# Where the bias products, the weights and the first strips stand in a four-layer network of involutions and convolutions

## The chip, the cores and the metric

The kernel runs on one core of one Trainium2 chip. The metric is the device time of one execution of the whole program, in microseconds (us), as the median of several runs. A core has TensorE (PE in the profile), VectorE (DVE), ScalarE (ACT), GpSimd (POOL) and SyncE (SP). Each takes its instructions in order from a queue of its own; ScalarE, GpSimd and SyncE also issue the DMA transfers here. PSUM holds what TensorE computes until another engine has read it ("evicted" it).

## The reference, cut to what matters

Four layers work on `x`, (4, 256, 56, 56) in fp32. Each normalizes its input and adds its result to it.

```python
x = x + L0(_gn(x))   # involution, 7x7, 16 groups
x = x + L1(_gn(x))   # two 3x3 convolutions
x = x + L2(_gn(x))   # involution, 7x7, 16 groups
x = x + L3(_gn(x))   # gate from Fourier transforms

def _gn(v, G=32, eps=1e-5):            # 32 groups of 8 channels
    g = v.reshape(B_, G, C_ // G, H_, W_)
    return ((g - mean(g)) / jnp.sqrt(var(g) + eps)).reshape(v.shape)

def L0(x):                             # one 7x7 filter for every pixel
    h = einsum('bchw,oc->bohw', x, reduce_w) + reduce_b        # 256 -> 64
    kern = einsum('bchw,oc->bohw', h, span_w) + span_b         # 64 -> 16 * 49
    return (kern * patches(x, 7, 7)).sum(over the 49 taps)

def L1(x):
    h = relu(bn(conv3x3(x, w1), ...))
    return relu(x + bn(conv3x3(h, w2), ...))

def L2(x):                             # as L0, with batch norms and ReLU
    t = relu(bn1(einsum('bchw,oc->bohw', x, w1)))
    wgt = einsum('bchw,oc->bohw', t, w2) + b2
    return relu(bn2((wgt * patches(x, 7, 7)).sum(over the 49 taps)))
```

## The kernel before

**Tiles.** A unit is one image and one half of the channels: 128 channels on the partitions, 56 x 56 pixels. There are eight units, taken in order. All four layers are one program. Layers 0 and 2 come from `involution_layer`, layer 1 from `conv_layer`; layer 3 is folded into layer 2's pass. The tile scheduler is bound to the order of the program text on each engine by `in_order`, so instructions of one engine run as the text issues them.

**An involution's unit.** `bottleneck` (for the first image of layer 0: `begin`) computes the 64 values `h` for each pixel: products of the image with `redn`, the reduction weights times the norm's scale (L459, in layer 0 L529), evicted by ScalarE into `hp` with the bias `hb` (L478, L566). The bias comes from a small product of `red_sb`, the unscaled weights, with the norm's shift (L437). Then `tap_matrices` makes a banded matrix for each group: 32 groups of 36 products (L580). Every third group is evicted by ScalarE (L591, with bias tables `zb_sb`), the others by VectorE (L598). The loop has *hooks*: after group n, the listed steps of other work are issued. Last, `apply` multiplies, for each of 7 columns of pixels, the matrices with the windows of the image (L622).

The windows come from `next_strip` and `next_windows`. `next_strip` normalizes a column's strip of the image into the only `strip_sb`: GpSimd in layer 0 (L381), ScalarE in layer 2 (L379). `next_windows` transposes it on TensorE (seven products, L396), ScalarE copies the result (L408), and SyncE and GpSimd issue copying DMAs (L414, L416). At the first unit of a layer three columns are made ahead of `apply`. Before, the first strip is issued after `bottleneck`, and the pairs of window and next strip at hooks 2, 7 and 12 of the matrices.

**The start of layer 0 (`begin`).** The images' first two halves are loaded by SyncE. The biases `sb` of the filters, the span weights and `red_sb` are loaded by GpSimd's queue. `window_biases` turns the biases into the table `zb_sb`: 24 products of 16 columns each (L255) and a copy by ScalarE (L262). Then come the first half's statistics (VectorE) and norm, `norm_steps`: aggregate the statistics (L204), average over 8 channels by a product with `gavg` (L207, twice), scale and shift. `warm` issues products whose results nobody reads. Products of the first half (L529, 0) go ahead of the second half's norm, those of the second half follow. The 20 evictions by L566 come next, then the matrices.

**The start of layer 1.** The convolutions are computed in a transformed domain: along x, six positions k for four outputs. `row_weights` makes the six weight sets from the three columns of the filter, in two halves of the input channels; per half there are three operations on VectorE for the sums and differences (u2, u1, u2) and three for the positions 3 and 4 (u4, u3, u4). It is a generator: each `next` issues one part. `weights1` is the first convolution's, `weights2` the second's. `phases` (L1290, ScalarE) normalizes a chunk of rows, `transform` (L1293 to L1317, VectorE) makes the six inputs, and `load_rows` loads the next chunk's rows. At the start of the layer the order on each engine is:

- VectorE: the six operations of sums and differences, four steps of the transform, the six other weight operations, the eight remaining steps;
- TensorE: 24 products of `window_biases` for layer 2 (L255), then the convolution (L1411);
- ScalarE: eight phases, then the copy of the bias table.

**The pass of layer 1.** Twelve chunks of rows (three of each image) go through the first convolution (`conv1`: L1411, or L1382 for positions 1 to 3 of all chunks but the first) and the second (`conv2`: L1493) in the order (1,0), (1,1), (2,0), (1,2), (2,1) and so on. Each chunk has a list `after` of what VectorE and ScalarE are to do behind which position: the transform of the next chunk's input (`input2` ends at L1318), outputs and sums. The five parts of `weights2` are placed in the first two chunks; `(2, 0)` is the chunk that first reads them. The last chunk's list calls `begin_last`, which loads the first image of layer 2.

**The start of layer 2.** `red_sb` is a tile of each involution layer's own pool, and in layer 2 it is loaded by ScalarE's queue (L317) when that pool opens, which is after the convolutions. `bottleneck(0)` scales it into `redn`, makes `hb` and the products, and the matrices follow.

Of the kernel before, what the change touches and what calls it, by code (L numbers as in the profile page):

```python
# [10 lines left out]
F32 = mybir.dt.float32  # L11
# [5 lines left out]
P = 128  # L17
# [54 lines left out]
def net_kernel(  # L72
# [59 lines left out]
    for i in range(2):  # L132
        nc.scalar.dma_start(rp[i * R : (i + 1) * R, :], rpar)
    mhalf = const.tile([P, NB], F32, name="mhalf")
# [89 lines left out]

    def mark():
        return len(nc.cur_bb.bb.instructions)
# [23 lines left out]
    def window_biases(zb_sb, bias, ps):  # L250

        bias_f = bias[:G, KK * KK : KK * KK + ZN]
        for p in range(TP):
            z0 = ZF - p // TX * QX - p % TX
            nc.tensor.matmul(  # L255
                ps[:Q, p * G : (p + 1) * G],
                bias_f[:, z0 : z0 + Q],
                ident_sb[:G, :G],
                start=True,
                stop=True,  # L260
            )
        nc.scalar.copy(  # L262
            zb_sb.rearrange("q g p -> q p g"), ps[:Q, : TP * G].rearrange("q (p g) -> q p g", g=G)
        )
# [15 lines left out]
    def involution_layer(layer, xin, xout, red, span, sb, xs_of, ahead=None, pending=None):  # L280

        with ExitStack() as es:
# [12 lines left out]
            def warm(n, by):  # L295

                ps = one_bank()
                for _ in range(n):
                    nc.tensor.matmul(ps[:, :P], ident_sb, by, start=True, stop=True)
# [11 lines left out]

            red_sb = wpool.tile([P, NB, 2, R], F32, name="red_sb")

            def load_red():
                for i in range(2):
                    eng = nc.gpsimd if layer == 0 else nc.scalar
                    eng.dma_start(red_sb[:, :, i], red.rearrange("(cb p) r -> p cb r", p=P))  # L317

            if layer == 2:
                load_red()  # L320
# [41 lines left out]
            def next_strip():  # L362

                if len(strips) == len(columns):
                    return
                b, cb, tx = columns[len(strips)]
                rstd, shift = (t[:, cb : cb + 1] for t in norms[layer][b])
                st = strip_sb
                strips.append(st)
                lo, hi = max(0, tx * TX - PAD), min(W, tx * TX + TX + PAD)  # L370
                at = lo - (tx * TX - PAD)
                if at > 0:
                    nc.vector.memset(st[:, PAD : PAD + H, 0:at], 0.0)
# [47 lines left out]
            def bottleneck(b):  # L421
# [64 lines left out]
            def begin():  # L486
# [4 lines left out]
                biases = bias_table(scratch[:, n:], sb, nc.gpsimd.dma_start, nc.scalar.copy)  # L491
# [3 lines left out]
                load_red()  # L495
# [9 lines left out]
                redn = work.tile([P, NB, 2, R], F32, name="redn", bufs=1)  # L505
                rstd, shift = norms[0][0]
                steps(sums0, NCHUNK)
                norm = norm_of(0, 0, 0, sums_of[0, 0])
                steps(norm, 2)
                warm(4, ident_sb)  # L510
                steps(norm, 2)
                warm(8, ident_sb)
# [7 lines left out]


                pairs = [two_banks() for _ in range(4)]
                bank = pairs[3][:, 1, :]
# [34 lines left out]
                for j in range(NH):  # L558
                    products(j, 1)
                for j in range(NH):  # L560
# [3 lines left out]
                    for py in range(min(rows, TY)):  # L564
                        dst = hp[:, py, :, a0 : a0 + n, :]
                        nc.scalar.activation(dst, s[:, py, :, :n, :], AF.Identity, bias=hb)  # L566
                return folds
# [587 lines left out]
    def conv_layer(xin, xout, st, ahead):  # L1155
        with ExitStack() as es:
# [44 lines left out]
            def row_weights(u, wc, raw=None):  # L1201
# [520 lines left out]
```

## Time and profile before

| | |
|---|---|
| median of 3 runs | 1817.9 us (1817.29 to 1822.03) |
| the profiled execution | 1812.46 us |
| its span | 1810.7 us |
| mean granted clock of TensorE | 0.979 |
| busy: TensorE, VectorE, ScalarE, GpSimd | 1720.8, 1375.4, 842.2, 430.0 us |
| products of the matrices, L580, and of the windows, L622 | 392.1 and 379.0 us |
| products of the second convolution, L1493 | 385.0 us |
| products of the first convolution, L1411 and L1382 | 212.3 and 98.6 us |
| layer 0 | 0 to 507 us |
| layer 1 | 507 to 1240 us |
| layers 2 and 3 | 1240 to 1811 us |

The span is that of one profiled execution, from its first instruction to its last; the runs are other executions of the same program, without a profile. Busy times of different engines overlap. The clock is what the chip granted TensorE: 1.00 is full speed, 0.50 half of it. The layers' bounds are read from the timeline: the first product of layer 1's biases starts at 507.1 us, the last product of the second convolution ends at 1240.2 us.

### The profile page before, as it was taken

What the parts mean: (1) busy time and instruction counts of PE and PEld (TensorE: products, weight loads), DVE (VectorE), ACT (ScalarE), POOL (GpSimd) and SP (SyncE); (2) the same over time, 40 slices, a digit from 0 to 9 for tenths busy, and PEclk for the clock granted to TensorE, in tenths of its full rate; (3) what the DMA queues carried; (4) which work ended last, traced back from release to release, by engine and by line L of the source; (5) the groups of instructions that cost most, each with busy time, mean ns of one, the idle gap of its engine ahead of it and who ended that gap; (6) DMA issues with size and microseconds to landing.
All of it is one profiled execution on the core that took longest, in us unless ns stands there. A gap on an engine that the chain in (4) does not pass through costs nothing.

```text
span 1810.7 us, 55835 instructions
## 1 busy us (share of the span) xinstructions
PE 1720.8 (95%) x24034; PEld 1514.9 (84%) x24034; DVE 1375.4 (76%) x2729; ACT 842.2 (47%) x1981; POOL 430.0 (24%) x626
## 2 busy tenths in 40 slices
PE   7999999999989999999999999997999999899988
PEld 6998989889878988998899889985988887887876
DVE  3787777776689988898889888875777677677775
ACT  3566556555532322322232222113767567577564
POOL 2333433245210000000000000000000374563572
PEclk9999999999989999999999999998999999999997
DMA  2545534454651201120121111031534566665653
GB/s 85 158 154 165 164 119 143 159 159 116 209 174 49 69 26 63 63 70 30 59 73 59 41 60 34 34 135 49 161 132 149 168 218 188 202 210 168 169 156 127
DMA packets 66004, 215.77 MB, mean 119 GB/s; under 512 B 13237, under 2 KB 20926, under 8 KB 62046
## 3 DMA queue, kind: packets, MB, share of 16 engines
q1 hardware_dynamic: 48718, 145.24, 25.7%
q0 software_dynamic: 14688, 64.78, 11.3%
q8 instruction: 190, 3.11, 0.7%
q10 hardware_dynamic: 2352, 2.18, 0.4%
q14 instruction: 56, 0.46, 0.1%
HBM read 76.30 MB, written 49.15 MB: 69 GB/s over the span
## 4 chain that ended last, share of the span: by engine, by line
PE 76%; DVE 9%; ACT 6%; DMA 4%; issue 2%; POOL 2%; SPq 1%; ACTq 0%; POOLq 0%; DVEq 0%
PE mm L1493 19%; PE ps L580 18%; PE ps L622 14%; PE mm L1411 10%; PE mm L1382 5%; PE ps L396 5%; DMA xw<-xw 4%; ACT kt L591 3%; PE ps L459 2%; DVE un L642 1%; DVE kt L598 1%; ACT xw L408 1%; ACT hp L478 1%; SPq L414 1%; DVE res L1486 1%
## 5 line engine op out<-in xcount | busy, mean ns | idle before, releaser
L580 PE MATMUL ps<-hp,z_sb 64*126 64x133 f32 x6144 | 392.1, 281 | 16.2 <-ACT kt L591 7.0
L622 PE MATMUL ps<-kt,xw 126*32 126x48 f32 (+1 forms) x12544 | 379.0, 236 | 24.1 <-DMA xw<-xw 12.1
L622 PEld LDWEIGHTS ps<-kt,xw 126*32 126x32 f32 (+1 forms) x12544 | 341.9, 122 | 68.2 <-issue 46.3
L580 PEld LDWEIGHTS ps<-hp,z_sb 64*126 64x126 f32 x6144 | 369.1, 187 | 34.6 <-ACT kt L591 12.7
L598 DVE TENSOR_TENSOR kt<-ps,zb_sb 126x798 f32<-126x798 f32 x336 | 319.8, 981 | 90.1 <-PE ps L580 89.5
L1493 PE MATMUL mm<-v,u_sb 128*128 128x280 f32 (+1 forms) x1728 | 385.0, 385 | 3.4 <-DVE v L1318 3.4
L1493 PEld LDWEIGHTS mm<-v,u_sb 128*128 128x128 f32 x1728 | 327.9, 190 | 57.5 <-DVE v L1318 3.8
L591 ACT ACTIVATE kt<-ps,zb_sb 126x133 f32<-126x133 f32 x1056 | 306.9, 442 | 96.2 <-PE ps L580 95.6
L1411 PE MATMUL mm<-v,u_sb 128*128 128x252 f32 (+1 forms) x936 | 212.3, 388 | 3.4 <-DVE v L1302 3.4
L1411 PEld LDWEIGHTS mm<-v,u_sb 128*128 128x128 f32 x936 | 178.3, 192 | 33.8 <-issue 3.5
L1530 POOL DMA_DIRECT2D x<-xs x24 | 13.1, 546 | 683.2 <-DVE xs L1529 427.4
L642 DVE SCALAR_TENSOR_TENSOR un<-ps,s,un 128x240 f32<-128x240 f32 x224 | 102.5, 457 | 85.7 <-ACT un L637 81.5
L642 DVE SCALAR_TENSOR_TENSOR un<-ps,par_sb,un 128x240 f32<-128x240 f32 x224 | 98.3, 457 | 87.1 <-ACT un L635 82.8
L1478 ACT ACTIVATE res<-xs,shift,norm_sb 128x1120 f32<-128x1120 f32 (+1 forms) x24 | 30.2, 1259 | 236.3 <-DVE xs L1529 107.3
L408 ACT COPY xw<-ps 126x896 f32<-126x896 f32 x112 | 101.4, 906 | 47.9 <-PE ps L396 37.7
L647 POOL TENSOR_TENSOR xs<-un,xs 128x240 f32<-128x240 f32 x112 | 72.3, 664 | 192.4 <-DVE un L642 192.3
L396 PE MATMUL ps<-ident_sb,strip_sb 128*126 128x128 f32 x784 | 111.7, 283 | 6.1 <-POOL strip_sb L381 5.8
L635 ACT ACTIVATE un<-ps,par_sb 128x240 f32<-128x240 f32 x112 | 50.1, 448 | 115.7 <-PE ps L622 113.4
L1382 PE MATMUL mm<-xs,u_sb 128*128 128x126 f32 (+1 forms) x792 | 98.6, 277 | 1.3 <-DVE xs L1345 0.9
L396 PEld LDWEIGHTS ps<-ident_sb,strip_sb 128*126 128x126 f32 x784 | 84.9, 142 | 17.0 <-POOL strip_sb L381 6.9
L637 ACT ACTIVATE un<-ps,bn_t,s 128x240 f32<-128x240 f32 x112 | 60.0, 538 | 83.3 <-PE ps L622 72.1
L1382 PEld LDWEIGHTS mm<-xs,u_sb 128*128 128x128 f32 x792 | 94.5, 191 | 2.4 <-issue 1.0
(254 smaller groups left out, 1925.8 us busy)
## 6 DMA issues: line engine op xcount, KB each, us to landing
xw<-xw SPq DMA_DIRECT2D x168, 252.0 KB
xw<-xw SPq DMA_DIRECT2D x224, 126.0 KB
xw<-xw POOLq DMA_DIRECT2D x56, 252.0 KB, 4.7
xs<-x SPq DMA_DIRECT2D x24, 560.0 KB
x<-xs POOLq DMA_DIRECT2D x8, 1568.0 KB, 8.2
xs<-x SPq DMA_DIRECT2D x8, 1568.0 KB
xs<-in_x_dram SPq DMA_DIRECT2D x6, 1568.0 KB
x<-xs SPq DMA_DIRECT2D x6, 1568.0 KB
```

Of the source, the lines that this page charges most:

```text
L396: nc.tensor.transpose(ps[:Q, k * P : (k + 1) * P], flat[:, k * Q : (k + 1) * Q], ident_sb)
L408: nc.scalar.copy(xw[:, :NSB, :], ps[:Q, : NSB * P].rearrange("q (n c) -> q n c", n=NSB))
L580: nc.tensor.matmul(ps[:Q, i, k * NT : (k + 1) * NT], z_sb[i * R : (i + 1) * R, cb * GB // 2 + gp, z0 : z0 + Q], hp[i * R : (i + 1) * R, py ...
L591: nc.scalar.activation(kt[:, g0 + i, pb, :, k], ps[:Q, i, k * NT : (k + 1) * NT], AF.Identity, bias=zb_sb[:, cb * GB + g0 + i, p0 + k : p0 ...
L598: nc.vector.tensor_tensor(kt[:, g0 : g0 + 2, pb], ps[:Q, :, : PB * NT].rearrange("q i (k t) -> q i t k", k=PB), zb_sb[:, cb * GB + g0 : cb ...
L622: nc.tensor.matmul(v[m * j : m * j + m, i, :, k * TP : (k + 1) * TP], xw[:, window(ty), m * j : m * j + m], kt[:, ng * j : ng * j + ng, :, ...
L637: nc.scalar.activation(part, o[0], AF.Identity, bias=bn["t4"][:, cb : cb + 1], scale=bn["s4"][ng][:, 0, cb : cb + 1])
L642: nc.vector.scalar_tensor_tensor(part, o[e], s, part, ALU.mult, ALU.add)
L647: nc.gpsimd.tensor_tensor(dst, u, dst, ALU.add)
L1382: nc.tensor.matmul(ps[:, co * m : (co + 1) * m], u[ci][:, co * P : (co + 1) * P], v2[:, e, : n // 2, ci * WT : (ci + 1) * WT], start=(ci = ...
L1411: nc.tensor.matmul(ps, u1_sb[:, ci, dy, k, co * P : (co + 1) * P], v[:, k, dy * NB + ci : (dy + n - 1) * NB + ci + 1 : NB, :], start=(j == 0),
L1493: nc.tensor.matmul(ps, u2_sb[:, ci, dy, k, co * P : (co + 1) * P], v[:, k, dy * NB + ci : (dy + n - 1) * NB + ci + 1 : NB, :], start=(j == 0),
```

## The change

In layer 0, `window_biases` becomes a generator that yields after each product. 14 of the 24 products stay ahead of the first norm. Ten are issued after the products of the second half (L529), and the copy into `zb_sb` after the evictions into `hp`. The four PSUM pairs are taken earlier, and the bias products use the part of the last pair's second bank behind its first columns. The biases are loaded by ScalarE's DMA queue instead of GpSimd's.

`red_sb` is now a tile of the pool of constants, loaded for layer 2 by SyncE's queue at the start of layer 1 (`begin_conv`). Its scaled copies `redn` are constants too, and those of layer 2's first image are made in `begin_last`.

In layer 2, the first strip is issued ahead of `bottleneck(0)`, and two pairs of window and next strip ahead of the matrices; the third pair is at hook 7. The first two strips are made by GpSimd.

In `row_weights` the first sums of both halves come first, then both subtractions as a part of their own, then the positions 3 and 4. It now has six parts instead of five. For the first convolution, the part with the subtractions is issued after three steps of the transform; the second convolution's parts are called at the same places as before, so that the last of them falls at the end of chunk (1, 1).

After the bias products at the start of layer 1 come three products of 448 columns whose results nobody reads, and `load_rows(1)` follows them; they read the tile that it overwrites.

```diff
+    red_sb = const.tile([P, NB, 2, R], F32, name="red_sb")
+
+    def load_red(red, eng):
+        for i in range(2):
+            eng.dma_start(red_sb[:, :, i], red.rearrange("(cb p) r -> p cb r", p=P))
+
+    def new_redn():
+        return const.tile([P, NB, 2, R], F32, name="redn")
...
+    redn_of = {}
+    def norm_weights(layer, b):
+        redn = redn_of[layer, b] = new_redn()
+        for ci in range(NB):
+            nc.vector.tensor_scalar_mul(redn[:, ci], red_sb[:, ci], norms[layer][b][0][:, ci : ci + 1])
@@ window_biases @@
                 start=True,
                 stop=True,
             )
+            yield
         nc.scalar.copy(
@@ involution_layer @@
-            red_sb = wpool.tile([P, NB, 2, R], F32, name="red_sb")
-
-            def load_red():
-                for i in range(2):
-                    eng = nc.gpsimd if layer == 0 else nc.scalar
-                    eng.dma_start(red_sb[:, :, i], red.rearrange("(cb p) r -> p cb r", p=P))
-
-            if layer == 2:
-                load_red()
@@ next_strip @@
-                if layer == 2:
+                if layer == 2 and len(strips) > 2:
                     nc.scalar.activation(dst, img, AF.Identity, bias=shift, scale=rstd)
                 else:
                     nc.gpsimd.tensor_scalar(dst, img, rstd, shift, ALU.mult, ALU.add)
@@ bottleneck @@
-                rstd, shift = norms[layer][b]
-                redn = work.tile([P, NB, 2, R], F32, name="redn", bufs=1)
-                for ci in range(NB):
-                    nc.vector.tensor_scalar_mul(redn[:, ci], red_sb[:, ci], rstd[:, ci : ci + 1])
+                _, shift = norms[layer][b]
+                if (layer, b) not in redn_of:
+                    norm_weights(layer, b)
+                redn = redn_of[layer, b]
@@ begin @@
-                biases = bias_table(scratch[:, n:], sb, nc.gpsimd.dma_start, nc.scalar.copy)
+                biases = bias_table(scratch[:, n:], sb, nc.scalar.dma_start, nc.scalar.copy)
...
-                window_biases(zb_sb, scratch[:, n:], one_bank())
+                pairs = [two_banks() for _ in range(4)]
+                bank = pairs[3][:, 1, :]
+                biases = window_biases(zb_sb, scratch[:, n:], bank[:, R:])
+                steps(biases, 14)
...
                 for j in range(NH):
                     products(j, 1)
+                steps(biases, TP - 14)
...
                         nc.scalar.activation(dst, s[:, py, :, :n, :], AF.Identity, bias=hb)
+                run(biases)
                 return folds
@@ the hooks of the first unit @@
                 nc.sync.dma_start(zb_sb, zb2_dram)
+                next_strip()
                 run(bottleneck(0))
                 hooks0[3] = list(pending[0])
-            next_strip()
-            for i in range(NXW):
-                hooks0.setdefault(2 + 5 * i, []).extend((next_windows, next_strip))
+                for _ in range(NXW - 1):
+                    next_windows()
+                    next_strip()
+                hooks0[7] = [next_windows, next_strip]
+            if layer == 0:
+                next_strip()
+                for i in range(NXW):
+                    hooks0.setdefault(2 + 5 * i, []).extend((next_windows, next_strip))
@@ begin_conv @@
         raw_weights(1, 0, 1, nc.sync)
+        load_red(red2, nc.sync)
@@ row_weights @@
                 for w0, w1, w2, u1, u2, u3, u4 in ws:
                     tt(u2, w0, w2, ALU.add)
                     tt(u1, u2, w1, ALU.add)
+                    yield
+                for w0, w1, w2, u1, u2, u3, u4 in ws:
                     tt(u2, u2, w1, ALU.subtract)
-                    yield
+                yield
@@ conv_layer @@
-            window_biases(zb2, room["bias"], one_bank())
+            run(window_biases(zb2, room["bias"], one_bank()))
             nc.sync.dma_start(zb2_dram, zb2)
+
+            ps = one_bank()[:, : CR * W]
+            for _ in range(3):
+                nc.tensor.matmul(ps, ident_sb, room["rows"][:, : CR * W], start=True, stop=True)
             load_rows(1, xin)
             g = input1(0)
-            for _ in range(4):
+            for _ in range(3):
                 next(g)
+            next(weights1)
+            next(g)
             run(weights1)
@@ begin_last @@
             load_block(blocks[0, cb], src[2][0][cb])
+        norm_weights(2, 0)
```

More of the change, by code (lines that the diff above doesn't have):

```diff
@@ L293, in one_bank, with warm @@
                 return two_banks()[:, 0, :]
-            def warm(n, by):
-                ps = one_bank()
+            def warm(n, by, ps=None):
+                if ps is None:
+                    ps = one_bank()
                 for _ in range(n):
@@ L494, in begin @@
                 next(tables)
-                load_red()
+                load_red(red, nc.gpsimd)
                 hp = new_h().rearrange("p (y x a t) -> p y x a t", y=TY, x=TX, t=NTX)
@@ L501, in begin @@
                 run(tables)
-                window_biases(zb_sb, scratch[:, n:], one_bank())
+                pairs = [two_banks() for _ in range(4)]
+                bank = pairs[3][:, 1, :]
+                biases = window_biases(zb_sb, scratch[:, n:], bank[:, R:])
+                steps(biases, 14)
                 folds = batch_norms()
                 sums0, sums1 = sums(0, 0), sums(0, 1)
-                redn = work.tile([P, NB, 2, R], F32, name="redn", bufs=1)
+                redn = new_redn()
                 rstd, shift = norms[0][0]
                 steps(sums0, NCHUNK)
-                norm = norm_of(0, 0, 0, sums_of[0, 0])
+                norm = norm_steps(sums_of[0, 0], lambda: bank, 0, 0, 0)
                 steps(norm, 2)
-                warm(4, ident_sb)
+                warm(4, ident_sb, pairs[3][:, 0, :])
                 steps(norm, 2)
-                warm(8, ident_sb)
+                warm(8, ident_sb, pairs[3][:, 0, :])
                 steps(norm, 1)
@@ L519, in begin @@
                 steps(sums1, NCHUNK - 4)
-                pairs = [two_banks() for _ in range(4)]
-                bank = pairs[3][:, 1, :]
                 norm = norm_steps(sums_of[0, 1], lambda: bank, 0, 0, 1)
```

## The prediction

> **What bounds the kernel now.** I read the page first, for the bound, and then the timeline and the windows at the four places that the diff touches.
>
> ```profile
> span 1810.7 us, 55835 instructions
> PE 1720.8 (95%) x24034; PEld 1514.9 (84%) x24034; DVE 1375.4 (76%) x2729; ACT 842.2 (47%) x1981; POOL 430.0 (24%) x626
> PE 76%; DVE 9%; ACT 6%; DMA 4%; issue 2%; POOL 2%; SPq 1%; ACTq 0%; POOLq 0%; DVEq 0%
> L1493 PE MATMUL mm<-v,u_sb 128*128 128x280 f32 (+1 forms) x1728 | 385.0, 385 | 3.4 <-DVE v L1318 3.4
> ```
>
> TensorE is the bound: what is saved where TensorE waits, or runs slowly, shifts all that follows it. The last line has the one wait of the second convolution, 3.4 us for VectorE (L1318).
>
> **A, the first norm.** The timeline of the first 45 us (start, length, engine, line):
>
> ```profile
> 1.50 0.69 POOL L244 DMA_DIRECT2D xs<-in_sb_dram  x1 [0.20 <-issue]
> 6.97 0.23 ACT L247 COPY xs<-xs 16x49 f32<-16x49 f32 x1 [2.58 <-DMA xs<-in_sb_dram]
> 7.26 10.42 PE L255 MATMUL ps<-ident_sb,xs 16*126 16x16 f32 x48 [7.26 <-ACT xs L247]
> 10.39 0.34 DVE L204 BATCH_NORM_AGGREGATE mv<-st 128x2 f32<-128x42 f32 x1
> 17.61 0.59 PE L207 MATMUL ps<-mv,gavg_sb 128*128 128x1 f32 x2
> 32.90 5.75 ACT L566 ACTIVATE hp<-ps,hb 128x168 f32<-128x168 f32 x20 [14.09 <-PE ps L529]
> 38.60 3.75 PE L580 MATMUL ps<-hp,z_sb 64*126 64x133 f32 x36 [2.15 <-ACT hp L566]
> ```
>
> The statistics are ready at 10.73, but their product L207 stands behind 24 bias products until 17.61. A bias product is two records, 10.42/24 = 0.434 us. The change leaves 14 ahead: 10 x 0.434 = 4.34 us less.
>
> It also moves the load of the biases from GpSimd's queue to ScalarE's, where it is issued after the table load and the copy that ends at 4.39, and waits for the first x transfer (its statistics began at 4.58). In that queue the trace's packets go strictly one transfer after the other: the last rp packets run to 8.0 to 8.2, and this load is behind them. Bounds: it lands as before (0) or some 2.2 us later, L247 at 9.2. I take 2.0, because the queue's packets show that order. GpSimd issues the span loads 0.69 us earlier; ScalarE's copies of them (8.84 to 12.1) slip at most 0.5 us, and nobody reads them until 38.6. The second half of x: one of its transfers now waits for cp, the next for rp, so they start some 1 us later; they landed by 14.2 and are first used at 20.44, which becomes 18.1. Hidden.
>
> The 10 others come after the products of L529, which end at 36.46. TensorE waits there until 38.60; at full clock a bias product is 0.22 us (507.1 to 510.3), so 2.2 us fill the 2.15. The copy into zb_sb (1.10 us, L262) now stands on ScalarE between hp and the first eviction, where 1.13 us were idle (39.78). Both covers are just long enough; without them it would be 2.2 and 1.1. **A: 4.34 - 2.0 = -2.3** (-4.3 to -0.7, the last if a window of half clock falls differently, 1.4).
>
> **B, the start of the convolutions.**
>
> ```profile
> 508.11 6.62 ACT L1290 ACTIVATE ph<-xs,norm_sb 128x294 f32<-128x294 f32 x8 [1.68 <-POOL xs L647]
> 515.44 0.80 DVE L1298 SCALAR_TENSOR_TENSOR v<-ph 128x616 f32<-128x616 f32 x1
> 517.93 37.19 PE L1411 MATMUL mm<-v,u_sb 128*128 128x280 f32 x144 [3.37 <-DVE v L1302]
> ...
> 510.33:513.74 3.41, 3.41 (x18) 3.41 (x18) 3.31 (x5) 3.41 (x5) 0.00 (x0) 0.50 1.04 421
> 520.57:523.98 3.41, 3.41 (x9) 2.50 (x8) 3.34 (x4) 0.07 (x1) 0.00 (x0) 0.50 0.36 147
> 523.98:527.40 3.42, 3.42 (x16) 2.71 (x16) 3.39 (x6) 0.32 (x1) 0.00 (x0) 1.00 0.02 5
> ```
>
> In the windows the last three columns are granted clock, DMA share, GB/s. The clock falls to half at 510.33, under the narrow bias products, and returns at 523.98, after one window filled with wide ones. The two subtractions (L1220, 0.985 us each) go behind L1302, but L1298 also needs ScalarE's last phase (514.73): it starts at 514.8, 0.65 us earlier, and everything behind the subtractions is 1.97 - 0.65 = 1.3 us later. The three wide products are 448 columns; L1411 has 280 in 0.934 us a pair at half clock, so 1.49 each, 4.5 us, ending at 518.9: TensorE starts some 1 us later, but with the clock back one window sooner, and is about 1.2 us earlier by 527. That is not kept: VectorE is busy 9.7 of 10 us here, the next conv1 chunk waits for its L1345 at 556.0, and on the way it has 0.41 and 0.96 us of waits for TensorE, which take up its 1.3. The load of the next rows now waits for the wide products, 2.4 us later; its reader waits at 527.97 for VectorE. **B: 0** (-0.3 to +1).
>
> A page speaks of this place otherwise. The Trainium skill (TensorE: Matmul & The Clock Gate, "HAM oscillation") says to allow no idle gaps over some 3.4 us; TensorE is listed as busy under the bias products and still loses the clock, so the measurement goes ahead of the rule. By the rule the wide products would run at full clock, and B would still be 0, VectorE being the bound.
>
> **D, the second convolution's weights.** Before, all twelve weight operations (0.95 to 0.985 us each) stand ahead of L1318, for which TensorE waits 587.2 to 590.87. After, three of them (those of the second half of the channels) are behind it: L1318 ends at 590.8 - 2.95 = 587.9. The product then needs the moved weights for its second half: they start after L1434 (591.86 - 2.95 = 588.9) and the needed one is done 1.94 later, 590.85. Three pairs of 0.377 run 587.95 to 589.1, three from 590.9 to 592.05. ScalarE's copy of that product is at 594.59 before. Of these 2.5 us, 1.4 depend on the window of half clock 592.25 to 595.66: bounds -1.1 to -3.1 with it and without. **D: -1.9**; L1440 and what follows on VectorE keep their times, as the number of operations is the same.
>
> **C, the start of the last involution.**
>
> ```profile
> 1243.13 0.99 ACTq L317 DMA_DIRECT2D red_sb<-in_red_dram  x2
> 1247.04 0.99 PE L437 MATMUL ps<-norm_sb,red_sb 128*128 128x1 f32 x4 [6.81 <-DMA red_sb<-in_red_dram]
> 1247.95 7.42 PE L459 MATMUL ps<-xs,redn 128*64 128x504 f32 x28
> 1251.47 8.34 ACT L478 ACTIVATE hp<-ps,hb,bn_s 64x168 f32<-64x168 f32 x20 [19.30 <-PE ps L459]
> 1259.64 4.36 PE L580 MATMUL ps<-hp,z_sb 64*126 64x133 f32 x36 [4.27 <-ACT hp L478]
> ```
>
> The weights are loaded when the place is free and land 4 us later. After, they and their scaled copy are there since the convolutions: two issues (0.99) on SyncE at 464, where it waits 15 us for its next (cover gone: +1), and two scalings (0.48) on VectorE in a chunk with slack. L437 then waits only for the last PSUM read, L1524, done at 1240.71; products 1240.8 to 1247 run beside VectorE, at full clock, since the 6.8 us gap is gone. What is late next is the bias hb on VectorE: L1529 ends at 1244.40, two norm steps 0.14, memset 0.20, hb 0.22: 1245.1 against ScalarE's 1251.47, so -6.35. GpSimd's first strip (0.89) runs then too; L547 took 0.85 us beside L381 where its equal L516 took 0.28, so up to 0.57 back, I take 0.25: -6.1.
>
> The matrices up to 1289.7 are 30.1 us. TensorE's own work in them is 32 groups of 0.738 (60 records in 3.69) and four sets of transposes of 0.98: 27.5, so 2.6 are lost to half clock and waits. After, two sets stand ahead of it: 25.6. Two strips leave ScalarE (0.93, 1.04), but two window copies and a strip (0.91, 0.91, 1.04) are now queued ahead of its first eviction, which comes 1.3 us later after hp than before. Loss 0 to 3.9; I take 2.6 again, the nearest row: 28.2, -1.9. GpSimd's last output DMA goes 0.9 us later, read 300 us after. **C: -8.0** (-6.4 to -10.8).
>
> Against C stands the skill's same page, "PE-mode transpose": transposes do not count as busy for the clock. No row here shows them alone. By it the 14 transposes would not hold the clock and the loss would be nearer 3.4: C -7.2.
>
> **Sum:** -2.3 + 0 - 1.9 - 8.0 = -12.2. The profiled execution took 1812.46 us (span 1810.7 and 1.76 around it), which gives 1800.3. Its time is 5.4 under the median of 1817.9; I take the sum from the median: **1805.7**.
>
> **Rivals.** R1, the gains are partly given back: A -1.0, B +1.0, D -0.5 (the wait moved to the weights), C -6.4: -6.9, 1811.0. For it: ScalarE is busy 25.0 of 30.1 us in the matrices, VectorE 9.7 of 10 in B. Against it: the cover rows above. R2, slower: in the last involution TensorE starts the matrices at half clock, ScalarE's late evictions keep opening gaps, and no 3.41 us window is full, so that the clock does not return. A group costs 1.43 instead of 0.738; all 32 give +20 on C, 1825.7; it decides from 18 groups on (12.2/0.69). For it: at the end of the kernel the page shows PEclk 7 in the last slice. Against it: 36 records at half clock were enough twice (39.3 to 42.7, 1257.8 to 1264.7) to bring it back, as TensorE at half clock is itself the bound. R3, the change does not do what it says: L437 still waits for something of the convolution until 1247; C is the 0.5 of the scalings: -4.7, 1813.2. The order of the built program speaks against it.
>
> **Chances.** Forecast 0.72, R1 0.14, R3 0.06, R2 0.08. About 0.3% (5.5 us) is what a measurement can tell from no change; the runs before span 0.26%. Faster: 0.72 and 0.08 of R1, 0.80; same: R3 and the rest of R1, 0.12; slower: R2, 0.08. The best bounds give -18, the worst without a rival -6; with R1 and R3 inside and R2 left out: 1800 to 1814.
>
> **What would show it.** A: L207 near 15.3 and L580 near 36.4. B: L1411 at about the same distance from the bias products, clock back a window sooner, L1382 not earlier than A brings it. D: L1493's wait for L1318 under 1 us and a second one for the weights. C: no gap before L437, ScalarE's hp some 6 us earlier. Wrong would be a later L580 in A (the bias load), or half clock for more than two windows after hp in C.

## The result, and the profile after

| | before | changed |
|---|---|---|
| median of 8 runs each | 1818.01 us (1814.48 to 1826.22) | 1812.55 us (1806.19 to 1815.32) |
| profiled execution | 1812.46 us | 1815.32 us |
| ratio of the runs | | 0.9962, 95% interval 0.9942 to 0.9981 |

The change saves 5.5 us by the medians and 6.9 by the ratio (3.5 to 10.5 by its interval); 12.2 were forecast. One execution of both_again (below) took 9300 us, far from the other five, and is left out of the figures. The two profiled executions alone would mislead: that of the kernel before is faster than each of its eight runs, that of the changed kernel is its slowest. So I read the traces stage by stage. Times are from the span's start, in us.

| | before | changed | difference |
|---|---|---|---|
| first matrices of layer 0 start | 38.60 | 44.09 | +5.5 |
| layer 0's last window product ends | 505.90 | 511.10 | +5.2 |
| second convolution starts | 582.64 | 586.87 | +4.2 |
| its second chunk starts | 641.38 | 643.56 | +2.2 |
| convolutions end | 1240.23 | 1242.39 | +2.2 |
| first eviction into `hp`, layer 2 | 1251.47 | 1247.09 | -4.4 |
| first window products, layer 2 | 1289.63 | 1281.52 | -8.1 |
| end of the span | 1810.70 | 1813.55 | +2.9 |

In the changed program the line numbers are 10 to 22 higher: L255 is L273, L207 L217, L299 (the warming products) L319, L529 L540, L566 L578, L580 L593, L1493 L1515, L1318 L1340, L437 L447, L459 L469, L478 L488. In the kernels of the experiments some are a few lines higher still (L1518 and L1511 are L1515 and L1508 here).

**A** went the wrong way. The timeline of the changed kernel (start, length, engine, line; in brackets the idle time before it and what ended it):

```profile
4.82 0.35 ACTq L262 DMA_DIRECT2D xs<-in_sb_dram  x1
10.80 0.23 ACT L265 COPY xs<-xs 16x49 f32<-16x49 f32 x1 [6.41 <-DMA xs<-in_sb_dram]
11.09 6.14 PE L273 MATMUL ps<-ident_sb,xs 16*126 16x16 f32 x28 [11.09 <-ACT xs L265]
17.16 0.59 PE L217 MATMUL ps<-mv,gavg_sb 128*128 128x1 f32 x2
17.61 2.05 PE L319 MATMUL ps<-ident_sb 128*128 128x128 f32 x8
19.70 0.16 DVE L220 COPY gm<-ps 128x1 f32<-128x1 f32 x1 [8.31 <-PE ps L319]
20.94 3.56 PE L319 MATMUL ps<-ident_sb 128*128 128x128 f32 x16
24.54 0.16 DVE L148 TENSOR_SCALAR norm_sb<-ps 128x1 f32<-128x1 f32 x1 [4.09 <-PE ps L319]
...
34.06 7.24 PE L540 MATMUL ps<-xs,redn 128*128 128x504 f32 x14 [0.39 <-DVE hb L568]
41.23 2.37 PE L273 MATMUL ps<-ident_sb,xs 16*126 16x16 f32 x20
43.63 0.51 ACT L578 ACTIVATE hp<-ps,hb 128x56 f32<-128x56 f32 x2 [0.59 <-PE ps L273]
44.09 3.22 PE L593 MATMUL ps<-hp,z_sb 64*126 64x133 f32 x30 [0.49 <-ACT hp L578]
```

The biases' load is issued at 4.82 and its reader starts at 10.80, against 6.97 before. Its 16 packets of 196 bytes ran from 8.55 to 9.64 (before 5.37 to 6.20), behind those of `rp`, which ended at 8.87, much as the prediction had it; but its reader came 1.2 us after the last of them. The fourteen products give back what the load lost (L217 at 17.16, before 17.61). But then VectorE's copy of the average waits, not for the average, done at 17.75, but for L319, the first four warming products (two records each), which nobody reads; the second time it is the eight others, for which L148 waits until 24.54, while before it started at 20.36. The last eviction, too, waits for bias products that it does not read. The warming products, the averages, the bias products and the last rows' products (7th of seven) now all lie in one PSUM tile of two banks.

**D** and **C** went as forecast or better. The waits of TensorE from 586 to 644 us (line, what it waited for, total, times, longest):

```profile
PE mm L1515 <- DVE u_sb L1246: 1.5, 1, 1.5
...
PE mm L1515 <- DVE v L1340: 0.4, 1, 0.4
```

The 3.4 us for the transform have become 0.4, and 1.5 for the weights that were moved behind it. The start of layer 2 in the timeline:

```profile
1243.02 0.58 PE L447 MATMUL ps<-norm_sb,red_sb 128*128 128x1 f32 x4 [0.63 <-DVE xs L1546]
1243.52 5.92 PE L469 MATMUL ps<-xs,redn 128*64 128x504 f32 x28
1246.75 0.20 DVE L383 MEMSET strip_sb<- 128x168 f32 x1
1246.87 0.10 DVE L458 SCALAR_TENSOR_TENSOR hb<-ps,bn_s,bn_t 128x1 f32<-128x1 f32 x1
1247.09 8.33 ACT L488 ACTIVATE hp<-ps,hb,bn_s 64x168 f32<-64x168 f32 x20 [12.76 <-DVE hb L458]
...
1252.30 0.96 PE L406 MATMUL ps<-ident_sb,strip_sb 128*126 128x128 f32 x7 [1.64 <-ACT hp L488]
...
1255.26 7.46 PE L593 MATMUL ps<-hp,z_sb 64*126 64x133 f32 x96 [2.00 <-ACT hp L488]
...
1280.61 0.98 PE L406 MATMUL ps<-ident_sb,strip_sb 128*126 128x128 f32 x7
```

The gap of 6.8 us ahead of L447 is 0.63. ScalarE now waits for the bias `hb`, which stands on VectorE's queue behind the strip's edge (L383). The matrices take 25.4 us up to the last set of transposes (L406 at 1280.61), against 29.1.

### The profile page after: what moved, and what is told of

It reads as the page before. It is cut to its first block, busy times and chain, and to the rows that moved or that the text cites. A ratio compares the mean times of both kernels' runs of the same rounds, so it can differ in the third digit from the quotient of the medians.

```text
span 1813.6 us, 55844 instructions
## 1 busy us (share of the span) xinstructions
PE 1723.7 (95%) x24040; PEld 1514.2 (83%) x24040; DVE 1376.3 (76%) x2729; ACT 840.2 (46%) x1979; POOL 430.8 (24%) x627
## 3 DMA queue, kind: packets, MB, share of 16 engines
q1 hardware_dynamic: 49262, 145.37, 25.6%
## 4 chain that ended last, share of the span: by engine, by line
PE 73%; DVE 12%; ACT 5%; DMA 4%; issue 3%; POOL 2%; SPq 1%; POOLq 0%; ACTq 0%; DVEq 0%
PE mm L1515 18%; PE ps L593 18%; PE ps L635 14%; PE mm L1433 9%; PE mm L1404 5%; PE ps L406 5%; DMA xw<-xw 3%; ACT kt L604 2%; DVE un L655 2%; PE ps L469 1%; DVE kt L611 1%; DVE res L1508 1%; DVE xs L1367 1%; SPq L424 1%; ACT xw L418 1%
## 5 line engine op out<-in xcount | busy, mean ns | idle before, releaser
L635 PE MATMUL ps<-kt,xw 126*32 126x48 f32 (+1 forms) x12544 | 381.1, 236 | 31.9 <-issue 20.2
L635 PEld LDWEIGHTS ps<-kt,xw 126*32 126x32 f32 (+1 forms) x12544 | 342.4, 122 | 77.5 <-issue 54.2
L593 PE MATMUL ps<-hp,z_sb 64*126 64x133 f32 x6144 | 391.3, 281 | 10.1 <-ACT kt L604 6.1
L593 PEld LDWEIGHTS ps<-hp,z_sb 64*126 64x126 f32 x6144 | 369.6, 187 | 27.7 <-ACT kt L604 12.0
L1515 PE MATMUL mm<-v,u_sb 128*128 128x280 f32 (+1 forms) x1728 | 383.5, 383 | 1.9 <-DVE u_sb L1246 1.5
L1515 PEld LDWEIGHTS mm<-v,u_sb 128*128 128x128 f32 x1728 | 326.1, 189 | 56.3 <-DVE u_sb L1246 1.9
L406 PE MATMUL ps<-ident_sb,strip_sb 128*126 128x128 f32 x784 | 113.6, 286 | 8.3 <-POOL strip_sb L391 5.2
L406 PEld LDWEIGHTS ps<-ident_sb,strip_sb 128*126 128x126 f32 x784 | 86.6, 144 | 19.3 <-POOL strip_sb L391 8.3
```

Source lines behind the costliest of these rows:

```text
L406: nc.tensor.transpose(ps[:Q, k * P : (k + 1) * P], flat[:, k * Q : (k + 1) * Q], ident_sb)
L593: nc.tensor.matmul(ps[:Q, i, k * NT : (k + 1) * NT], z_sb[i * R : (i + 1) * R, cb * GB // 2 + gp, z0 : z0 + Q], hp[i * R : (i + 1) * R, py ...
L635: nc.tensor.matmul(v[m * j : m * j + m, i, :, k * TP : (k + 1) * TP], xw[:, window(ty), m * j : m * j + m], kt[:, ng * j : ng * j + ng, :, ...
L1515: nc.tensor.matmul(ps, u2_sb[:, ci, dy, k, co * P : (co + 1) * P], v[:, k, dy * NB + ci : (dy + n - 1) * NB + ci + 1 : NB, :], start=(j == 0),
```

## The experiments

The ratio is to runs of the kernel before on the same chip, with its 95% interval. The stages are compared in the traces, one execution each. In programs that are equal up to there, the first matrices of layer 0 start within 0.5 us of each other (35.99 to 36.49), but layer 0 ends within 1.9 (501.81 to 503.67); the later parts vary more, as the last experiment shows. The runs were taken on several chips, and the intervals of most of these kernels overlap: the parts are told apart by the stages, not by the medians.

| | median | ratio |
|---|---|---|
| a_undone | 1806.21 | 0.9930 (0.9910 to 0.9950) |
| warm_other_pair | 1807.62 | 0.9937 (0.9917 to 0.9957) |
| load_gpsimd | 1809.87 | 0.9948 (0.9927 to 0.9968) |
| both_mended | 1801.39 | 0.9906 (0.9883 to 0.9929) |
| both_again, the same program | 1807.50 | 0.9930 (0.9908 to 0.9953) |
| m_no_idle | 1804.15 | 0.9931 (0.9907 to 0.9954) |
| m_old_strips | 1799.91 | 0.9915 (0.9881 to 0.9948) |
| m_strips_act | 1803.25 | 0.9937 (0.9915 to 0.9960) |
| m_red_late | 1807.27 | 0.9932 (0.9906 to 0.9958) |
| m_old_w2 | 1807.48 | 0.9935 (0.9909 to 0.9961) |
| m_plus | 1800.55 | 0.9926 (0.9900 to 0.9952) |
| m_hb_first | 1795.47 | 0.9869 (0.9841 to 0.9897) |

### The start of layer 0 as before (a_undone)

```diff
-                bias_table(scratch[:, n:], sb, nc.scalar.dma_start, nc.scalar.copy)
+                bias_table(scratch[:, n:], sb, nc.gpsimd.dma_start, nc.scalar.copy)
...
-                steps(biases, 14)
+                run(window_biases(zb_sb, scratch[:, n:], one_bank()))
...
-                warm(8, ident_sb, pairs[3][:, 0, :])
+                warm(8, ident_sb)
```

> The changed kernel with the start of layer 0 as it was before (biases on GpSimd's queue, all 24 products ahead of the first norm); B, C and D stay. Theory W (the start of layer 0 costs 5.5 us, as the stage times of the two traces have it): the first matrices start at 38.6 instead of 44.1 us, and the median is 5.5 us under the changed kernel's, about 1807. Rival P (the forecast's -2.3 holds and the profiled execution of the changed kernel was only an unlucky one): the median is 2.3 us above the changed kernel's, about 1815.

The matrices start at 39.70 us, 4.4 earlier than in the changed kernel, and layer 0 ends 5.3 earlier (505.83). The median is 6.3 us under the changed kernel's 1812.55, near theory W's 1807 and not rival P's 1815. A did cost about what its stage shows; the forecast's -2.3 falls. The start is still 1.1 later than in the kernel before (38.60), where 38.6 was expected; the eight warming products took 3.76 us instead of 3.00.

### The warming products in another pair (warm_other_pair)

```diff
-                warm(4, ident_sb, pairs[3][:, 0, :])
+                warm(4, ident_sb, pairs[0][:, 0, :])
...
-                warm(8, ident_sb, pairs[3][:, 0, :])
+                warm(8, ident_sb, pairs[0][:, 0, :])
```

> The changed kernel, but the products of warm(), whose results nobody reads, are written into the first PSUM pair instead of the last, which also holds the first norm's small products. Theory W: VectorE's copy of the first average (L220) waits for the four warming products and its L148 for the eight only because they share a tile. With the tile apart, L220 starts at 17.8 instead of 19.7, L148 at about 20.3 instead of 24.5; the products of the first half then stand behind the eight warming products, so that they start at about 23.7 instead of 26.07. Matrices start 2.4 us earlier, 4.1 if the window of half clock in the second half's products goes too. Rival L (the late load of the biases is all of the loss): no change within 0.3 us at the first matrices.

```profile
17.69 0.16 DVE L220 COPY gm<-ps 128x1 f32<-128x1 f32 x1 [6.39 <-PE ps L217]
19.82 0.16 DVE L148 TENSOR_SCALAR norm_sb<-ps 128x1 f32<-128x1 f32 x1 [1.40 <-PE ps L228]
...
23.06 3.55 PE L540 MATMUL ps<-xs,redn 128*128 128x504 f32 x8
...
30.95 5.54 PE L540 MATMUL ps<-xs,redn 128*128 128x504 f32 x14 [0.39 <-DVE hb L568]
```

Both readers now wait for the averages alone. The first products of L540 start at 23.06 instead of 26.07, and the matrices at 39.29, 4.8 us earlier. It is the shared tile, and rival L falls. But only 3.0 of the 4.8 are the wait. Another 1.7 are the second half's products, 5.54 us instead of 7.24: in the changed kernel a window of half clock (34.39 to 37.80, with a granted clock of 0.50) fell into them, and here none did. Where such a window falls is not the edit's (see the last section). At the end of layer 0, 4.4 are left (506.74).

### The load on GpSimd's queue again (load_gpsimd), and both together (both_mended)

```diff
-                bias_table(scratch[:, n:], sb, nc.scalar.dma_start, nc.scalar.copy)
+                bias_table(scratch[:, n:], sb, nc.gpsimd.dma_start, nc.scalar.copy)
```

> The changed kernel, but the load of the biases is on GpSimd's queue again. Theory W: the first bias product starts at 7.3 instead of 11.1 us, the average L217 at 13.4 instead of 17.2, and all behind it is 3.8 us earlier; L220 and L148 still wait for the warming products. Rival S (the sharing of the PSUM tile is all of the loss, since the second half's images set the pace anyway): the first matrices start less than 0.5 us earlier.

The first bias product starts at 7.16 and L217 at 13.24, as expected, and L540's first at 22.35, 3.7 us earlier. At the matrices (42.40) only 1.7 is left: the first half's eight products took 5.68 us instead of 3.65, and the second half's 7.24 in both, with a window of half clock in them. At the end of layer 0 nothing is left (511.59 against 511.10), so what the load alone is worth further on is not shown.

> The changed kernel with both: the load on GpSimd's queue and the warming products in the first pair. Theory W: 6.2 us earlier at the first matrices (37.9), up to 7.9 if a window of half clock goes; that is 0.7 to 2.4 us before the kernel before, and near the forecast's -2.3. The median is 1805 to 1806.5. Rival: the gains overlap, since with the load early the first half's statistics (11.0) and TensorE's warming set the pace, and the two together give no more than 4.

The matrices start at 36.15 us: 7.9 before the changed kernel, the upper end of what was expected, and 2.45 before the kernel before. At the end of layer 0 it is 8.8 and 3.6 (502.35). The rival, no more than 4, falls. The median, 1801.39, is below the 1805 to 1806.5 expected, but the same program run again has 1807.50: that the mended start is better than the old one of a_undone (1806.21) is seen in the stages, not in the medians. The timeline of both_mended:

```profile
13.11 0.59 PE L217 MATMUL ps<-mv,gavg_sb 128*128 128x1 f32 x2
13.55 2.06 PE L319 MATMUL ps<-ident_sb 128*128 128x128 f32 x8
13.73 0.16 DVE L220 COPY gm<-ps 128x1 f32<-128x1 f32 x1 [3.31 <-PE ps L217]
...
15.87 0.16 DVE L148 TENSOR_SCALAR norm_sb<-ps 128x1 f32<-128x1 f32 x1 [1.40 <-PE ps L228]
...
24.30 0.16 DVE L148 TENSOR_SCALAR norm_sb<-ps 128x1 f32<-128x1 f32 x1 [1.44 <-PE ps L540]
...
35.69 0.51 ACT L578 ACTIVATE hp<-ps,hb 128x56 f32<-128x56 f32 x2 [0.58 <-PE ps L273]
```

L220 now starts when the average is done, beside the warming products. Two waits of the same kind are left: L148 of the second norm waits for a product of L540 that it does not read (the kernel before has this one too, at 29.09), and the last eviction for the bias products.

### Those two taken out (m_plus)

```diff
-                products(6, 0)
                 steps(norm, 2)
+                products(6, 0)
...
-                for j in range(NH):
+                for j in [NH - 1] + list(range(NH - 1)):
                     products(j, 1)
-                steps(biases, TP - 14)
-                for j in range(NH):
+                for j in [NH - 1] + list(range(NH - 1)):
```

The bias products left then run behind the evictions in the program's text.

> The kernel both_mended with two more waits on the shared tile taken out at the start of layer 0: the first half's product into the last pair (2 rows) is issued behind the second norm's average, so that L148 no longer waits for it (1.4 us idle, 1.1 of them after the average is done), and the small last part of the second half's products and evictions comes first, so that the last eviction no longer waits for the ten bias products (0.6). Theory W: the first matrices start 1.7 us earlier (34.4), 3.4 if the window of half clock in the second half's products goes too. Rival: ScalarE's evictions set the pace there; less than 0.6 earlier.

The matrices start at 34.38, 1.77 us earlier than in both_mended, as theory W has it. In the median the two can't be told apart.

### The idle products at the start of the convolutions (m_no_idle)

```diff
-            for _ in range(3):
-                nc.tensor.matmul(ps, ident_sb, room["rows"][:, : CR * W], start=True, stop=True)
```

> The kernel both_mended without the three wide products at the start of the convolutions, whose results nobody reads. Forecast theory P: what they bring (the clock back a window sooner) is not kept, since VectorE sets the pace; from the end of the last apply of layer 0 to the first product of the second convolution 75.7 us stays within 0.3. Rival K: it is kept, and the stretch becomes 76.7, as in the kernel before.

The stretch took 76.05 us: within P's bound, at its edge. The next chunk, the first of the second convolution, took 57.40 instead of 56.64, where its wait fell into a window that lost the clock. But the same program without an edit (both_again, below) has 76.05 too, and others with equal code here have up to 77.25. What the three products bring is within the spread; it is not settled. The windows of half clock at this place show what the spread goes with: the clock stays at half for four windows (13.7 us) in the kernel before and in m_no_idle, and for two or three in the changed kernel and in most others that have the three products, where the stretch takes 75.7 to 76.2 us. In the two of equal code where it stays at half for four all the same (m_strips_act, m_red_late), it takes 77.2.

### The last involution's start, part by part

```diff
-                if layer == 2 and len(strips) > 2:
+                if layer == 2:
```

This is m_strips_act; m_old_strips has besides it the hooks of the kernel before.

> The kernel both_mended with layer 2's first strips and windows as before: all strips on ScalarE, the three columns at hooks 2, 7 and 12 of the first matrices. The early weights stay. Theory M: the moved columns bring what the traces show, 25.4 against 29.1 us in the first matrices and 0.98 of transposes behind; ScalarE's first eviction into hp keeps its distance of 4.7 us to the last convolution product, and the first matrices with the transposes behind them become 3.7 us longer than 26.3. Rival T: only the two sets of transposes (2.0) are moved, and the rest came with the clock after the weights' wait: 2.0 longer.

From the last convolution product to the first window product: 42.13 us, both_mended 39.15, before 49.40. The matrices with the transposes behind them became 4.2 us longer (30.43), M rather than T. But ScalarE's first eviction came 1.33 us sooner, at 3.37 instead of 4.70 behind the last convolution product. So at the first window product the moved strips are worth 3.0 net, with 1.3 lost at `hb`; the medians (1799.91, both_mended 1801.39 and 1807.50) do not show it.

> The kernel both_mended with the first two strips of layer 2 on ScalarE instead of GpSimd, at the same places in the program. Theory Q (the engine matters, not the place alone): the second strip stands on ScalarE behind the 20 evictions into hp and the first window copy, TensorE's second set of transposes waits for it ahead of the matrices, and these start about 3 us later (13.0 to 16 us after the last convolution product). Rival R (the place alone matters): the matrices start within 0.5 us of the same distance.

The matrices start 16.63 us behind the last convolution product instead of 12.89: 3.7 later. Q holds; on ScalarE the moved strips lose more than the place brings (first window product at 42.90 us, m_old_strips 42.13).

```diff
-        load_red(red2, nc.sync)
-        norm_weights(2, 0)
+            if layer == 2:
+                load_red(red, nc.scalar)
```

> The kernel both_mended with the last involution's reduction weights loaded by ScalarE's queue when layer 2 opens and scaled there, as before the change; the moved strips stay. Theory M: the products of the first bottleneck wait for the load again, ScalarE's first eviction into hp comes 11.2 us after the last convolution product instead of 4.7, and the matrices start 6.3 us later than 12.9. Rival V: VectorE's own end of the convolutions is close behind the load, so that less than 4 come back.

The first eviction came 8.90 us behind the last convolution product, 4.2 later than in both_mended, and the edit did not do what it was to do. The rows by tile (duration least, median and most in ns, first and last start in us) and by timeline:

```profile
L139 ACTq DMA_DIRECT2D red_sb<-in_red_dram x2: 378/537/696, 379.5 to 379.9; - x2
```

```profile
1240.22 0.86 DVE L241 TENSOR_SCALAR redn<-red_sb,norm_sb 128x128 f32<-128x128 f32 x2
1240.96 8.24 PE L471 MATMUL ps<-xs,redn 128*64 128x504 f32 x28 [3.97 <-DVE redn L241]
```

The load went out at 379.5 us, long before layer 2: its tile is among the constants now and not in the layer's pool. Only the scalings were late, behind the last residual on VectorE. So 4.2 us are the scalings' place alone. That is V's mechanism, a little above its bound of 4; M's 6.5 did not come. The other 2.3 of the 11.24 before would then be the load's; that was not tried alone.

### The second convolution's weights in the old order (m_old_w2)

```diff
                     tt(u1, u2, w1, ALU.add)
+                    if by_half:
+                        tt(u2, u2, w1, ALU.subtract)
                     yield
```

> The kernel both_mended with the second convolution's weights made in the old order (the three sums and differences of one half of the channels after the other, all twelve operations ahead of L1318's counterpart). Theory D: the first chunk of the second convolution waits 3.4 us for VectorE's transform again, and takes 58.7 us to the start of the next chunk's instead of 56.6. Rival: the shorter wait came from the clock alone (no window of half clock in this chunk of both_mended), and the chunk stays under 57.2.

```profile
PE mm L1518 <- DVE v L1343: 3.5, 1, 3.5
```

The whole wait is back, and the chunk takes 59.79 us (before 58.74, both_mended 56.64). D holds: the wait comes from the order. The chunk's time has a part of the clock besides: two windows of half clock fall into it here (586.39 to 593.22), one before, none in both_mended. With one window each, the new order (m_no_idle, 57.40) is 1.3 us shorter than the old one (before, 58.74).

### The bias hb ahead of the first strip (m_hb_first)

```diff
+                first = bottleneck(0)
+                next(first)
+                next(first)
                 next_strip()
-                run(bottleneck(0))
+                run(first)
```

> The kernel m_plus with layer 2's first strip issued after the bottleneck's bias hb instead of ahead of the bottleneck. Theory O: hb waits on VectorE behind the strip's memset of its edge, which waits for the norm and for the end of the last residual; ahead of it hb runs in a gap 1.6 us earlier, as in m_old_strips (1236.41, 0.6 after the product). ScalarE's first eviction into hp comes 3.4 us after the last convolution product instead of 4.7, and the matrices start 1.2 us earlier with their short length of 26.3 kept. Rival: the first strip then is late, TensorE's transposes wait, and the matrices start at the same time.

```profile
1234.28 0.22 DVE L458 SCALAR_TENSOR_TENSOR hb<-ps,bn_s,bn_t 128x1 f32<-128x1 f32 x1 [0.28 <-PE ps L447]
...
1236.40 8.38 ACT L488 ACTIVATE hp<-ps,hb,bn_s 64x168 f32<-64x168 f32 x20 [11.43 <-DVE res L1511]
...
1237.77 0.20 DVE L383 MEMSET strip_sb<- 128x168 f32 x1
```

`hb` is ready long before ScalarE begins. The first eviction comes 3.37 us behind the last convolution product, the matrices start 1.3 sooner and end with the first window product at 37.33 (m_plus 39.31). Theory O holds; what ScalarE waits for now is the last residual on VectorE (L1511). This kernel has the lowest median of the study, and its interval lies wholly under that of the changed kernel. It overlaps with that of both_mended, though, and the 2.0 us of this stage are less than what its median is under that of m_plus (5.1, of four and five runs), so the rest is not explained.

### The same program twice (both_again)

> The kernel both_mended itself once more, without an edit, to see what two profiled executions of the same program differ in. Theory N (layers 2 and 3 vary by themselves, by waits of TensorE on window copies): the stages up to the first matrices of layer 2 agree within 1.5 us, and the time from there to the end differs from 524.3 by several us. Rival G (the spread between the kernels is theirs, set by the phase at which layer 2 starts): it agrees within 1 us.

Up to the first window product of layer 2: 1273.82 us against 1272.67. From there to the end: 537.43 against 524.25. N holds. TensorE's largest waits in that stretch, both_mended first, then both_again:

```profile
PE ps L635 <- DMA xw<-xw: 11.6, 8, 4.0
PE ps L635 <- issue: 7.3, 9, 2.9
```

```profile
PE ps L635 <- issue: 13.9, 10, 2.9
PE ps L635 <- DMA xw<-xw: 9.8, 11, 1.4
```

L635 are the window products (L622 before); "issue" is a wait for nothing that the profile shows. The two sum to 18.9 and 23.7 us. The rest of the 13.2 is in part the clock, 20.5 against 27.3 us at half speed up to the last window product, which is worth half of the difference, 3.4; some 5 us stay open. So the -8.1 at 1281.52 is a better mark of the change than the +2.9 of the spans, and the interval of the ratio (-10.5 to -3.5) holds it.

A rival is left. From the first window product to the end the traces take 516.56 us (m_old_strips), 521.07 (before) and 521.97 (m_strips_act) in the three kernels where ScalarE makes all strips of layer 2, and 523.48 to 537.43 in the eleven others. Whether the first strips on GpSimd cost something later on, or these three executions were lucky, no experiment settles.

## Why the prediction was right or wrong

The time lay in the range, and the sign was right; the size was about half of the forecast's, and for a reason that it did not have. That it lay in the range is partly luck: the range reaches up to 1814 for the rivals R1 and R3, which did not happen, and the other parts made up 3.4 us of what A lost. (The bounds of A to D add up to -18.5 and -7.2, and not to the -18 and -6 of the prediction.)

- **A**, forecast -2.3, measured +5.5 at the first matrices. Two terms failed. "I take 2.0" for the load: it was 3.8 (the reader at 10.80 against 6.97), outside the bounds of 0 to 2.2; with only the queue changed the first product moved by 3.9 (11.09 against 7.16). And the list of what the change adds had no wait for the PSUM pairs that are taken earlier: the warming products were moved into the tile that the norm's averages are read from, and that cost 3.0 us of waiting by itself, 4.8 with the window of half clock that fell behind it. Of the covers, the one at the first eviction was long enough (1.32 us from the first matrix product, before 1.18); the one at TensorE was not, as the last eviction waits for the ten bias products (0.6). The step "10 x 0.434" held: fourteen took 6.14, 0.439 each.
- **B**, forecast 0, measured -1.0 (76.74 to 75.77 us), not to be told from the 75.7 to 77.3 of programs that are equal here. The clock did come back sooner, as forecast (at half from 515.67 to 522.50, before from 510.33 to 523.98). That VectorE swallows the gain is not shown; that the stretch is longest among equal programs where the clock stays at half longest speaks rather against it.
- **D**, forecast -1.9, measured -2.1, with the second wait where it was expected. m_old_w2 brings the first wait back. The waits account for 1.5 of it (3.4 against 0.4 and 1.5); before, a window of half clock fell into this chunk, after, none did.
- **C**, forecast -8.0, measured -10.3. The bias `hb` was what came late next, and ScalarE's first eviction moved by 6.5 (forecast 6.1). The mis-sized term is the loss in the matrices: 2.6 was taken from the matrices before, and it is 0.7 (26.3 us from the first matrices to the first window product, 1255.26 to 1281.52, for 25.6 of TensorE's own). The Trainium skill (TensorE: Matmul & The Clock Gate, "PE-mode transpose") would have made it some 3.4 by the prediction's estimate, since it says that transposes do not count as busy in the same way; no run here had transposes alone, but that loss did not come.
- **The sum** to layer 2's first window product is -8.1 instead of -12.2: A is 7.5 worse there, B, C and D together 3.4 better. R1 has nearly the measured time, but not its places: it took C at -6.4 and A at -1.0. R2 and R3 did not happen: L447 waits 0.63 us, and no more than one window of half clock follows `hp`.

## What to carry to other kernels

When products are moved into a PSUM tile that something else is read from, list the tile's readers: here VectorE's copies and ScalarE's last eviction waited for the tile's earlier writers, also for those that wrote parts they do not read, and the twelve idle products in that tile cost 3.0 us of waiting that they did not cost in another. A load that is moved behind other transfers is priced by when its reader started last time and how much later it is issued (here 3.8 us later for an issue 3.3 later), not by when the queue looks empty. And two single executions are compared by stages; the difference of their spans can lie mostly in a stage that varies by itself.

## What the runs showed of the hardware

The windows of half clock do not stand at the same place of a program. The windows view of both_mended, then of both_again (us; busy PE, PEld, DVE, ACT and POOL with counts; granted clock, DMA share, GB/s):

```profile
26.12:33.20 7.08, 7.08 (x14) 3.17 (x14) 0.17 (x1) 3.57 (x12) 0.00 (x0) 0.76 0.01 2
...
36.00:42.00 6.00, 5.85 (x89) 5.59 (x91) 3.45 (x12) 5.53 (x16) 1.33 (x2) 1.00 0.06 16
```

```profile
26.12:33.20 7.08, 6.24 (x19) 3.17 (x19) 1.16 (x4) 3.55 (x13) 1.40 (x2) 1.00 0.01 2
...
36.00:42.00 6.00, 6.00 (x63) 5.59 (x65) 2.53 (x10) 3.92 (x10) 0.00 (x0) 0.72 0.01 3
```

The same program lost the clock in the products of layer 0 in one execution and in its first matrices in the other; the first matrices took 25.8 and 27.4 us. The Trainium skill (TensorE: Matmul & The Clock Gate, "The HAM clock gate") says that the window in which activity is counted runs free and does not start with the kernel, and these rows agree: one program, two places. It limits what an edit of 1 us at such a place can be shown to do.
